# A two-layer transformer kernel on one core: the value products of its second attention done by expert, with scattered and gathered rows

## The chip, the core and the metric

The kernel runs on one core of a Trainium2 chip. The core has five engines that work side by side, each strictly through its own list of instructions: TensorE (PE, with the loading of its stationary operand shown apart as PEld), VectorE (DVE), ScalarE (ACT), GpSimd (POOL) and SyncE (SP, which issues most of the DMA transfers). The metric is the device time of one launch in microseconds (us). Runs of the same kernel stand within some tenths of a per cent of each other. Beside the plain runs there is one profiled execution, from which the views in this document come.

## The reference, cut to what matters

The input `x` has 4 sequences (`b`) of 1024 tokens with 128 numbers. Two layers follow, each of which normalizes its input and adds two branches to it. The change is in the second branch of the first layer, an attention of 8 heads with 8 experts for the values and 8 for the outputs in each head:

```python
gate_v = _get_sel_gate(x, sel_v_w, rs)      # [b, s, 8 heads, 8 experts], two experts not zero per token and head
gate_o = _get_sel_gate(x, sel_o_w, rs)
q = einsum('bsd,hpd->bhsp', x, q_w);  k = einsum('bsd,hpd->bhsp', x, k_w)
xv = einsum('bsd,hedp->bshep', x, v_w)      # every token through all 8 experts of every head
v = einsum('bshep,bshe->bhsp', xv, gate_v)  # of which the gate keeps two
att = softmax(einsum('bhqp,bhkp->bhqk', q, k) * SCALE)
ctx = einsum('bhqk,bhkp->bqhp', att, v)
out = einsum('bshep,hepd->bsd', ctx[:, :, :, None, :] * gate_o[..., None], o_w)
```

`_get_sel_gate` takes a sigmoid of the routing logits, keeps the two largest of the eight per token and head, and divides them by their sum. The first branch of the layer is an attention of 16 heads that share one key and one value. The second layer has an attention with random features and a mixture of eight experts per token (two chosen) with a shared one.

## The kernel before

A batch's 1024 tokens lie as 8 tiles of 128 rows (`NT = 8`, index `n`). The first layer is one loop over 32 units `u` (batch `b`, head `h` of the second attention), each in eight steps `n`. In a step stand, in this order: the scores of token tile `n` against all keys and their softmax (`switch_softmax`: `ss` L676, the copy L679, the maximum L681, the exponential L683), the transposes of the tile before (`switch_transpose`: `pTp` L696, copied to `pTs` L700 by DVE and by ACT), up to two outputs (`switch_output`: `po` L729, eight experts weighted on DVE L733, added up by POOL L648, L649, L738 and L739, the last into `x`), and the values of the next unit (`switch_values`). The product of probabilities and values, `switch_context` (`cp`, L708), comes in two halves: the first at step 4, the second at step 0 of the next unit. Each of a unit's values must be ready before its first half.

`switch_values` makes the values of one token tile for all eight experts: two products of 128x512 on PE (`pv`, L659), a multiplication with the gates on DVE (`gv`, L663), and three additions on POOL that sum the experts (L648, L649, L668). Six of eight gates are zero.

Between these steps the first attention is woven in, as a generator (`first_attention`) that is advanced by a fixed number of its small steps per step of the unit (`attend`, `PACE`): `mx` L451, `sT` L505, `ov` L495 and the maximum `nmh` L457 on DVE. `row_ahead` prepares the next batch (`layernorm`, `switch_gates`) from a head's first step on. When a batch is complete, `router` of the second layer writes each token to two places of a DRAM tile `sorted_x`, one indirect DMA of 128 rows at a time (`xslot` L302 on DVE, the scatter L309 on POOL).

What sets the order: PE's instructions stand in the order in which the program is written. A scheduler orders the other engines, in the first layer SyncE too; in the second layer SyncE's order is the written one as well. Tiles of a pool with a tag are reused in turn: an instruction that writes a tile waits until those that used its buffer before are done, and two transfers that write the same DRAM tile wait for each other in turn.

Of the kernel before, what the change touches and what calls it, by code (L numbers as in the profile page):

```python
# [17 lines left out]
P = 128  # L18
# [21 lines left out]

FJ = 64
# [25 lines left out]
def two_layers(ctx: ExitStack, tc: tile.TileContext, a: dict, out: bass.AP):  # L67
# [7 lines left out]
    ctx.enter_context(tc.manual_schedule(engines={mybir.EngineType.PE}))  # L75
# [94 lines left out]

    nobody = fixed([P, 2, ROW], "nobody")
# [24 lines left out]
    def layernorm(layer, b, pool):  # L196

        mv = rt.tile([P, NT, 2], F32, tag="mv", name=f"mv{layer}_{b}")
# [6 lines left out]
        rstd = rt.tile([P, NT], F32, tag="rstd", name=f"rstd{layer}_{b}")  # L205
        nc.scalar.activation(rstd, mv[:, :, 1], AF.Sqrt, bias=eps_ln)
        nc.vector.reciprocal(rstd, rstd)
        moments[b] = mv, rstd
        for q in range(NT // 4):
            xn = pool.tile([P, 4, D], F32, tag="xn", name=f"xn{layer}_{b}_{q}")  # L210
# [41 lines left out]
    def router(b):  # L252
# [45 lines left out]
        mv, rstd = moments[b]  # L298
# [19 lines left out]
    with ExitStack() as l0:  # L318
# [6 lines left out]
        def switch_gates(b):  # L325
# [25 lines left out]
            m0, oh0, m1, oh1 = found  # L351
            den = pre.tile([P, ng], F32, tag="den", name=f"den{b}")
# [7 lines left out]
            weigh(to, oh0, m0, oh1, m1)  # L360
# [3 lines left out]
            )  # L364
            yield
# [4 lines left out]
        def mqa_prepare(b):  # L370
# [13 lines left out]
            for i in range(NPART):  # L384
                if i > 0:
                    nc.vector.tensor_tensor(qf, qf, qp, ALU.subtract)
                qp = at.tile([P, T], BF16, tag="qp0", name=f"qp0_{b}_{i}")
                nc.gpsimd.tensor_copy(qp, qf)
                nc.sync.dma_start(qd[i], qp)
                yield  # L390
# [92 lines left out]
        def mqa_values(b, g):  # L483
# [3 lines left out]
            for c in range(2):  # L487
# [13 lines left out]
                for kt in range(NT):  # L501
                    pTs = []
                    for i in range(4):
# [6 lines left out]
                            [P, 512], F32, tag="pT0", name=f"pT0_{b}_{g}_{c}_{kt}_{i}", bufs=12  # L510
# [10 lines left out]
                os_ = at.tile([P, 512], F32, tag="os0", name=f"os0_{b}_{g}_{c}", bufs=1)  # L521
# [16 lines left out]
        def mqa_out(b):  # L538
# [31 lines left out]
            yield from layernorm(1, b, pre)  # L570
# [33 lines left out]
        def switch_load(u):  # L604

            b, h = divmod(u, SH)
            vw = wst.tile([P, SE, P], F32, tag="vw", name=f"vw{u}")
            ow = wst.tile([P, SE, P], F32, tag="ow", name=f"ow{u}")
            if b == 0:
                qk = wst.tile([P, 2, P], F32, tag="qk", name=f"qk{u}")  # L610
                nc.sync.dma_start(qk[:, 0, :], a["q_wT"][:, ts(h, P)])
                nc.sync.dma_start(qk[:, 1, :], a["k_wT"][:, ts(h, P)])
                unit[u, "qk"] = qk
            nc.sync.dma_start(vw, a["v_w"][ts(h, SE)].rearrange("e d p -> d e p"))
            nc.sync.dma_start(ow, a["o_w"][ts(h, SE)].rearrange("e p d -> p e d"))
            unit[u, "w"] = vw.rearrange("d e p -> d (e p)"), ow.rearrange("p e d -> p (e d)")

        def switch_scores(u):
# [7 lines left out]
            qkT = sw.tile([P, 512], F32, tag="cTs", name=f"qkT{u}")  # L626
# [8 lines left out]
        def switch_queries(u):  # L635
            b, h = divmod(u, SH)
            qT = sw.tile([P, T], F32, tag="qTs", name=f"qTs{u}")
# [13 lines left out]
        def switch_values(u, n):  # L651
# [5 lines left out]
            for c in range(2):  # L657
                pv = small(f"pv{u}_{n}_{c}")
                nc.tensor.matmul(  # L659
                    pv, lhsT=xnT[b][:, ts(n, P)], rhs=unit[u, "w"][0][:, ts(c, 512)],  # L660
# [7 lines left out]
            nc.gpsimd.tensor_tensor(v[:, n, :], g[:, 0, :], g[:, 1, :], ALU.add)  # L668

# [34 lines left out]
        def switch_context(u, qg):  # L704
# [7 lines left out]
            cT = sw.tile([P, 512], F32, tag="cTs", name=f"cTs{u}_{qg}")  # L712
# [3 lines left out]
        def switch_output(u, n):  # L716
# [10 lines left out]
            for c in range(2):  # L727
                po = small(f"po{u}_{n}_{c}")
                nc.tensor.matmul(  # L729
                    po, lhsT=cT[:, ts(qt, P)], rhs=unit[u, "w"][1][:, ts(c, 512)],  # L730
# [13 lines left out]
        weights = (3.2, 2.2, 2.2, 1.8, 3.2, 2.2, 2.2, 1.8)  # L744
# [3 lines left out]
        VALUES = {1: (0,), 2: (1,), 3: (2, 3), **LATER}  # L748
# [5 lines left out]
        def row_ahead(b):  # L754

            yield from layernorm(0, b, pre)
# [4 lines left out]
        switch_load(0)  # L761
        run(layernorm(0, 0, pre))
# [5 lines left out]
        for b in range(1, B):  # L768
            load_x(b)
        steps = first_attention()  # L770
# [3 lines left out]
        for u in range(U + 1):  # L774
            b, h = divmod(u, SH)
            for n in range(NT):
# [18 lines left out]
                if u == 0 and n == 0:  # L795
                    switch_load(1)
                elif n == 5 and u + 2 < U and u > 0 or u == 0 and n == 7:
                    switch_load(u + 2 if u else 2)
# [8 lines left out]
                if u > 0 and 1 <= n <= 3:  # L807
                    switch_output(u - 1, n + 3)
                    if n == 3:
                        switch_output(u - 1, NT - 1)  # L810
                elif u < U and n >= 5:
# [3 lines left out]
                if u > 0 or n >= 4:  # L815
                    attend(0.3)
# [665 lines left out]
```

## Time and profile before

| | |
|---|---|
| median of 3 runs | 3563.88 us (3555.51 to 3567.87) |
| the profiled execution | 3553.15 us, its span 3551.4 us |
| mean granted TensorE clock | 0.970 |
| busy: PE, DVE, ACT, POOL | 94%, 71%, 46%, 47% of the span |
| last output of the first layer (`g_o`, L738) | 3025.8 us |
| `pv` L659 / `gv` L663 / POOL's first add L648 | 487.5 / 334.6 / 328.5 us busy |

A row of a group names the line, the engine, the operation, the tile written and those read, their shapes, how often, the busy time in us and the mean of one in ns, and behind the bar the time that the engine stood idle just before and what ended it. In the rows of PE a 128x512 product in fp32 has two records. In a timeline each row begins with the start and the length in us, and ends with the idle time ahead and its releaser in brackets. The chain is the work that ended last, followed back from the end.

### The profile page before, as it was taken

To read this page: it belongs to the slowest core of one execution; us is meant where nothing else is said; L and a number is where in the kernel's file an instruction comes from. 1 tells how busy PE (TensorE), PEld (TensorE's weight loads), DVE (VectorE), ACT (ScalarE), POOL (GpSimd) and SP (SyncE) were. 2 spreads that over 40 slices of the span, in tenths; PEclk is the share of its full clock that TensorE was granted. 3 is DMA by queue.
4 is the path that set the end of the run, shared out by engine and by line. 5 is a ranking of instruction groups with operands and counts; after the bars stand their busy time and mean duration, and the time that the engine had idled before them with its cause. 6 is when DMAs were issued, how large, how long until landed. Compare 5 with 4: busy or idle time off the path is not lost.

```text
span 3551.4 us, 41035 instructions
## 1 busy us (share of the span) xinstructions
PE 3339.5 (94%) x14270; PEld 1667.4 (47%) x14270; DVE 2522.9 (71%) x4598; ACT 1642.3 (46%) x2823; POOL 1661.9 (47%) x2204
## 2 busy tenths in 40 slices
PE   5999999999989998999989999999899999889996
PEld 2444444444444443444434444444444444457775
DVE  6876678767777768676877787677777675557774
ACT  2344443444445443444444434444454445345663
POOL 3644444444465455444455454444654443303334
PEclk9999999999999998999999999999999999898998
DMA  4530101000000000000000010000000000013346
GB/s 98 153 109 14 21 14 28 6 20 13 19 23 21 12 13 22 13 19 19 14 23 19 13 28 6 20 12 20 23 21 13 7 6 1 21 35 76 77 89 149
DMA packets 174851, 116.36 MB, mean 33 GB/s; under 512 B 11754, under 2 KB 162164, under 8 KB 174644
## 3 DMA queue, kind: packets, MB, share of 16 engines
q1 hardware_dynamic: 159124, 103.29, 10.6%
q0 software_dynamic: 13280, 9.38, 1.9%
q8 instruction: 113, 1.85, 0.2%
q10 hardware_dynamic: 2240, 1.07, 0.1%
q14 instruction: 94, 0.77, 0.1%
HBM read 77.20 MB, written 36.11 MB: 32 GB/s over the span
## 4 chain that ended last, share of the span: by engine, by line
PE 77%; DVE 13%; DMA 3%; POOL 3%; issue 2%; ACT 1%; SPq 1%; DVEq 0%; POOLq 0%; ACTq 0%
PE cp L708 12%; PE ss L676 11%; PE po L729 11%; PE pv L659 11%; PE ov L495 6%; PE sT L505 5%; PE pTp L696 5%; PE mx L451 5%; DMA sorted_x<-xslot,at_slot 3%; DVE nmh L457 2%; DVE nms L681 2%; PE pe L1344 2%; PE pb L1329 2%; PE qks L640 1%; DVE gv L663 1%
## 5 line engine op out<-in xcount | busy, mean ns | idle before, releaser
L457 DVE TENSOR_REDUCE nmh<-mx 128x1 f32<-128x512 f32 x1024 | 657.4, 680 | 340.4 <-PE mx L451 339.8
L648 POOL TENSOR_TENSOR g_o<-g_o 128x512 f32<-128x512 f32 x256 | 324.8, 1269 | 1226.7 <-DVE g_o L733 1005.9
L512 ACT ACTIVATE pT<-sT 128x512 f32<-128x512 f32 x1024 | 556.6, 601 | 414.3 <-PE sT L505 410.3
L659 PE MATMUL pv<-vw,xnT 128*128 128x512 f32 x1024 | 487.5, 609 | 18.0 <-DVE pTs L700 7.8
L676 PE MATMUL ss<-xnT,qTs 128*128 128x512 f32 x1024 | 494.4, 604 | 9.8 <-DVE gv L663 6.9
L708 PE MATMUL cp<-pTs,vs 128*128 128x512 f32 x1024 | 462.9, 606 | 38.8 <-DVE pTs L700 31.6
L729 PE MATMUL po<-ow,cTs 128*128 128x512 f32 x1024 | 474.7, 596 | 2.5 <-ACT ps L679 2.5
L679 ACT COPY ps<-ss 128x512 f32<-128x512 f32 x512 | 298.4, 587 | 361.9 <-PE ss L676 340.6
L681 DVE TENSOR_REDUCE nms<-ps 128x1 f32<-128x1024 f32 x256 | 310.7, 1214 | 185.9 <-ACT ps L679 185.2
L683 ACT ACTIVATE ps<-ps,nms 128x1024 f32<-128x1024 f32 x256 | 294.3, 1150 | 180.7 <-DVE nms L681 179.6
L663 DVE TENSOR_TENSOR gv<-pv,gates 128x512 f32<-128x512 f32 x512 | 334.6, 681 | 30.6 <-POOL x L739 10.3
L648 POOL TENSOR_TENSOR gv<-gv 128x512 f32<-128x512 f32 x256 | 328.5, 1283 | 34.2 <-DVE gv L663 34.1
L733 DVE TENSOR_TENSOR g_o<-po,go 128x512 f32<-128x512 f32 x512 | 328.4, 680 | 18.9 <-PE po L729 14.2
L708 PEld LDWEIGHTS cp<-pTs,vs 128*128 128x128 f32 x1024 | 193.6, 193 | 287.2 <-issue 230.4
L451 PE MATMUL mx<-ks,qs 72*128 72x512 bf16 x1024 | 311.8, 381 | 16.4 <-DVE gv L663 6.1
L505 PE MATMUL sT<-qs,ks 75*128 75x512 bf16 x1024 | 309.9, 384 | 7.8 <-ACT pT L512 2.3
L659 PEld LDWEIGHTS pv<-vw,xnT 128*128 128x128 f32 x1024 | 195.2, 194 | 244.0 <-issue 154.6
L696 PE MATMUL pTp<-ident,ps 128*128 128x128 f32 x2048 | 270.6, 275 | 17.9 <-ACT ps L683 11.8
L676 PEld LDWEIGHTS ss<-xnT,qTs 128*128 128x128 f32 x1024 | 191.8, 192 | 201.4 <-issue 131.3
L696 PEld LDWEIGHTS pTp<-ident,ps 128*128 128x128 f32 x2048 | 239.7, 141 | 90.4 <-issue 22.7
L729 PEld LDWEIGHTS po<-ow,cTs 128*128 128x128 f32 x1024 | 180.3, 191 | 158.4 <-issue 136.5
L495 PE MATMUL ov<-pT,va 128*32 128x512 f32 x2048 | 247.5, 598 | 0.0
(270 smaller groups left out, 3999.9 us busy)
## 6 DMA issues: line engine op xcount, KB each, us to landing
w<-in_w_dram SPq DMA_DIRECT2D x78, 256.0 KB
sorted_x<-nobody SPq DMA_DIRECT2D x16, 1040.0 KB
vw<-in_v_w_dram SPq DMA_DIRECT2D x32, 512.0 KB
ow<-in_o_w_dram SPq DMA_DIRECT2D x32, 512.0 KB
qs<-qd SPq DMA_DIRECT2D x144, 64.0 KB
xg<-sorted_x SPq DMA_DIRECT2D x39, 130.0 KB
sum<-nobody SPq DMA_DIRECT2D x8, 512.0 KB
y<-sum SPq DMA_DIRECT2D x16, 256.0 KB
```

The source lines that it names most:

```text
L451: nc.tensor.matmul(sc, lhsT=qs[0:NPAIR, i, ts(n, P)], rhs=ks[0:NPAIR, ts(kc, 512)], start=True, stop=True,)
L457: nc.vector.tensor_reduce(halves[:, i, n, kc : kc + 1], sc, axis=AX.X, op=ALU.max)
L495: nc.tensor.matmul(ov[32 * i : 32 * i + 32, :], lhsT=va[:, kt, :], rhs=pT, start=(kt == 0), stop=(kt == NT - 1),)
L505: nc.tensor.matmul(sc, lhsT=ks[:, ts(kt, P)], rhs=qs[:, i, ts(c, 512)], start=True, stop=True,)
L512: nc.scalar.activation(pT, sc, AF.Exp)
L648: nc.gpsimd.tensor_tensor(g[:, 0:4, :], g[:, 0:4, :], g[:, 4:8, :], ALU.add)
L659: nc.tensor.matmul(pv, lhsT=xnT[b][:, ts(n, P)], rhs=unit[u, "w"][0][:, ts(c, 512)], start=True, stop=True,)
L676: nc.tensor.matmul(sc, lhsT=qT[:, ts(n, P)], rhs=xnT[b][:, ts(c, 512)], start=True, stop=True)
L681: nc.vector.tensor_reduce(nm, p, axis=AX.X, op=ALU.max, negate=True)
L696: nc.tensor.transpose(pt[:, ts(k, P)], p[:, ts(4 * k4 + k, P)], ident)
L708: nc.tensor.matmul(cp, lhsT=v[:, kt, :], rhs=pT[:, kt, :], start=(kt == 0), stop=(kt == NT - 1),)
L729: nc.tensor.matmul(po, lhsT=cT[:, ts(qt, P)], rhs=unit[u, "w"][1][:, ts(c, 512)], start=True, stop=True,)
```

## The change

Units 0 and 1 keep the dense values. For the other 30, a token goes only through the two experts that its gate keeps:

- Once per batch, `places` counts for each head how many tokens each expert has, rounds that up to blocks of 128 slots (at most 23 blocks for a head, `NVB`), and gives each token its two slots. The slots and the two gate weights are kept in the part of `gates` that the gates of the values had. `rows_of_values` writes the normalized tokens as rows (`xv`).
- For each unit, `scatter` writes the 8 tiles of rows to their first and second slots in a DRAM tile `sorted_v` (16 indirect DMAs from POOL; four such tiles in turn, cleared once at the start). `PAIR` says how many in which step, for two units at a time.
- In six groups of up to four blocks, `group_load` reads the blocks back and loads for each block the 128x128 weights of its expert, whose number SyncE reads into a register; `group_turn` transposes the blocks on PE, `group_product` multiplies them on PE and stores the result to a DRAM tile `yv`.
- `gather` fetches for each token tile its two rows from `yv` (16 indirect DMAs from POOL into three buffers `yg`), and DVE adds them with their weights into the values `vs`.

SyncE's order in the first layer is the written one now. To make room, the buffers of `qTs`, `qp0` and `pT0` are fewer, and several tiles share tags (`xn`, `qkT`, `xvT` with `cTs`; `os0` with `pT0`). `row_ahead` begins at head 2 instead of 5, and the second layer's first normalization of a batch waits in the program until that batch's last output is written.

```diff
+NVB = 2 * NT + SE - 1
+VG = 4
+DENSE = 2
...
-    ctx.enter_context(tc.manual_schedule(engines={mybir.EngineType.PE}))
+    ctx.enter_context(
+        tc.manual_schedule(engines={mybir.EngineType.PE, mybir.EngineType.SP})
+    )
...
+    sorted_v = [
+        hbm.tile([NVB * P, D], F32, tag=f"sorted_v{i}", name=f"sorted_v{i}") for i in range(4)
+    ]
...
             m0, oh0, m1, oh1 = found
+            if b == 0:
+                yield from rows_of_values(0)
+            slots = pre.tile([P, ng], F32, tag="top_r", name=f"slots{b}")
+            slots = slots.rearrange("p (k n h) -> p k n h", k=2, n=NT)
+            yield from places(b, gates[b], oh1.rearrange("p (n g) e -> p n (g e)", n=NT), slots)
...
+        def rows_of_values(b):
+            xv = row_of[b] = sw.tile([P, NT, D], F32, tag="xv", name=f"xv{b}", bufs=1)
+            mv, rstd = moments[0, b]
+            for n in range(NT):
+                nc.vector.tensor_scalar(
+                    xv[:, n, :], x[b][:, n, :], mv[:, n, 0:1], rstd[:, n : n + 1],
+                    ALU.subtract, ALU.mult,
+                )
...
-                qp = at.tile([P, T], BF16, tag="qp0", name=f"qp0_{b}_{i}")
+                qp = at.tile([P, T], BF16, tag="qp0", name=f"qp0_{b}_{i}", bufs=1)
...
-                            [P, 512], F32, tag="pT0", name=f"pT0_{b}_{g}_{c}_{kt}_{i}", bufs=12
+                            [P, 512], F32, tag="pT0", name=f"pT0_{b}_{g}_{c}_{kt}_{i}", bufs=10
...
+            while b not in complete:
+                yield
+            yield from layernorm(1, b, sw)
...
+        def scatter(u, i):
+            n, k = divmod(i, 2)
+            nc.gpsimd.indirect_dma_start(
+                out=sorted_v[u % 4][:, :],
+                out_offset=bass.IndirectOffsetOnAxis(ap=column(u, k, n).bitcast(I32), axis=0),
+                in_=row_of[u // SH][:, n, :], in_offset=None,
+            )
...
+        def group_load(u, g):
+            m = min(VG, NVB - VG * g)
+            if g == 0:
+                plan(u)
+            xs = sw.tile([P, VG, D], F32, tag="xs", name=f"xs{u}_{g}", bufs=3)
+            rows = unit[u, "sorted"][ds(VG * P * g, m * P), :]
+            nc.sync.dma_start(xs[:, 0:m, :], rows.rearrange("(k p) d -> p k d", p=P))
+            wb = wst.tile([P, VG, P], F32, tag="vb", name=f"vb{u}_{g}", bufs=3)
+            for i in range(m):
+                j = VG * g + i
+                e = nc.sync.value_load(
+                    unit[u, "of"][0:1, j : j + 1], min_val=0, max_val=SH * SE - 1
+                )
+                nc.sync.dma_start(
+                    wb[:, i : i + 1, :], a["v_w"][ds(e, 1)].rearrange("e d p -> d e p")
+                )
...
+        def group_turn(u, g):
+            xs, _, m = unit[u, "g", g]
+            pt = small(f"xvT{u}_{g}")
+            for i in range(m):
+                nc.tensor.transpose(pt[:, ts(i, P)], xs[:, i, :], ident)
+            xT = sw.tile([P, 512], F32, tag="cTs", name=f"xvT{u}_{g}", bufs=3)
+            nc.scalar.copy(xT[:, 0 : m * P], pt[:, 0 : m * P])
...
+        def group_product(u, g):
...
+                nc.tensor.matmul(
+                    pv[:, ts(i, P)], lhsT=xT[:, ts(i, P)], rhs=wb[:, i, :],
+                    start=True, stop=True,
+                )
+            nc.scalar.copy(xs[:, 0:m, :].rearrange("p k d -> p (k d)"), pv[:, 0 : m * P])
+            rows = unit[u, "y"][ds(VG * P * g, m * P), :]
+            nc.sync.dma_start(rows.rearrange("(k p) d -> p k d", p=P), xs[:, 0:m, :])
+
+        def gather(u, n):
...
+            for k in range(2):
+                y = sw.tile([P, P], F32, tag="yg", name=f"yg{u}_{n}_{k}", bufs=3)
+                nc.gpsimd.indirect_dma_start(
+                    out=y[:, :], out_offset=None, in_=unit[u, "y"][:, :],
+                    in_offset=bass.IndirectOffsetOnAxis(
+                        ap=column(u, k, n).bitcast(I32), axis=0
+                    ),
+                )
+                w = column(u, 2 + k, n)
+                if k == 0:
+                    nc.vector.tensor_scalar(v, y, w, None, ALU.mult)
+                else:
+                    nc.vector.scalar_tensor_tensor(v, y, w, v, ALU.mult, ALU.add)
...
+        PAIR = (
+            (1, 1, 1, 1, 1, 1, 2, 2, 2, 1, 1, 1, 1, 0, 0, 0),
+            (1, 1, 1, 1, 1, 1, 0, 0, 0, 1, 1, 1, 1, 2, 2, 2),
+        )
...
+        for i in (2, 3, 0, 1):
+            nc.sync.dma_start(
+                sorted_v[i].rearrange("(k p) d -> p k d", p=P),
+                empty.unsqueeze(1).to_broadcast([P, NVB, D]),
+            )
...
+                if h == 2 and n == 0 and b + 1 < B:
+                    aside = row_ahead(b + 1)
...
-                if u + 1 < U:
-                    for i in ({4: range(4), **LATER} if u == 0 else VALUES).get(n, ()):
-                        switch_values(u + 1, i)
+                    for i in {4: range(4), **LATER}.get(n, ()):
+                        switch_values(1, i)
+                if u == 0 and 4 <= n:
+                    for i in range(4 * (n - 4), 4 * (n - 3)):
+                        scatter(2, i)
+                if u == 1:
+                    for i in range(3 * n, min(3 * n + 3, 2 * NT)):
+                        scatter(3, i)
+                odd = u % 2
+                v = u + 3 if odd else u + 2
+                if u > 0 and v < U:
+                    for k, counts in enumerate(PAIR):
+                        done = sum(counts[: n + 8 * (1 - odd)])
+                        for i in range(done, done + counts[n + 8 * (1 - odd)]):
+                            scatter(v + k, i)
+                NG_V = -(-NVB // VG)
+                v = u + 1
+                if DENSE <= v < U:
+                    if n == 0 and v == DENSE:
+                        group_load(v, 0)
+                        group_load(v, 1)
+                    if 1 <= n <= NG_V:
+                        group_product(v, n - 1)
+                    if n < NG_V:
+                        group_turn(v, n)
+                    if n + 2 < NG_V:
+                        group_load(v, n + 2)
+                    if n == 7:
+                        gather(v, 0)
+                        gather(v, 1)
+                if DENSE <= v + 1 < U and u > 0 and n >= 6:
+                    group_load(v + 1, n - 6)
+                if DENSE <= u < U and n < 3:
+                    gather(u, 2 * n + 2)
+                    gather(u, 2 * n + 3)
```

## The prediction, made before the changed kernel ran

> **What bounds the kernel now.** The page's busy shares and the chain come first, then the windows by stage, then the groups that the change touches, last the one row that resembles what it adds.
>
> ```profile
> PE 3339.5 (94%) x14270; PEld 1667.4 (47%) x14270; DVE 2522.9 (71%) x4598; ACT 1642.3 (46%) x2823; POOL 1661.9 (47%) x2204
> PE 77%; DVE 13%; DMA 3%; POOL 3%; issue 2%; ACT 1%; SPq 1%; DVEq 0%; POOLq 0%; ACTq 0%
> 1100.00:2500.00 1400.00, 1356.14 (x5172) 624.50 (x5171) 1023.08 (x1759) 644.39 (x1155) 698.60 (x915) 0.98 0.07 17
> L659 PE MATMUL pv<-vw,xnT 128*128 128x512 f32 x1024 | 487.5, 609 | 18.0 <-DVE pTs L700 7.8
> L663 DVE TENSOR_TENSOR gv<-pv,gates 128x512 f32<-128x512 f32 x512 | 334.6, 681 | 30.6 <-POOL x L739 10.3
> L648 POOL TENSOR_TENSOR gv<-gv 128x512 f32<-128x512 f32 x256 | 328.5, 1283 | 34.2 <-DVE gv L663 34.1
> ```
>
> In the window from 1100 to 2500 us (columns: PE, PEld, DVE, ACT, POOL busy, clock, DMA share, GB/s) PE works 97% of the time, DVE 73%, POOL 50%, ACT 46%: PE paces the first layer. The first layer's outputs end at 3025 us; with the start off, 32 units take about 92.3 us each, 11.5 us for each of a unit's eight steps. The values cost PE, DVE and POOL alike.
>
> **PE.** Removed per unit: 32 records of L659. In the PE timeline four of them start and the next group follows 1.71 us later, so 0.43 us a record, 13.7 us a unit (by the busy mean, which overlaps, more). Added: 23 transposes, eight of which follow at 0.87 to 1.09 us, so 2.7 us; 23 products of 128x128, two records each, by the row of `pe` (L1344: 81.7 us for 624 records) 0.26 us each, 6.0 us. Saved: about 5 us a unit, 30 units, 150 us. Where PE paces, a unit takes 87.5 us.
>
> **DVE and ACT.** DVE loses 16 `gv` of 681 ns (10.9 us) and gains 16 weighted sums of 128x128, priced by the `xslot` row (346 ns): 5.5 us. ACT gains 12 copies of 587 ns (L679): 7 us on 42. `places` adds some 35 DVE operations a batch of 0.2 to 0.35 us, about 10 us; DVE is idle 27% of the time and hides it after batch 0. None of these is late by its sum.
>
> **SyncE.** 23 `value_load`s (269, 152 and 18 ns) and as many weight loads (42, 29 and 378 ns): 0.9 us a block, 20 us a unit, with the group transfers 24. That fits in 87. They are loaded two groups ahead. An `xs` load waits in order on its scatters' landing, and queued behind it are `qs` loads for the first attention; I give that nothing at best and 2 us a unit at worst, and take nothing.
>
> **POOL.** Removed: eight add chains of 2.6 us a unit, 21 us. Kept: eight output chains, 3.17 us each (1028.36 to 1031.53 in the timeline), 25.4 us. Added: 16 scatters and 16 gathers, each issued by POOL. The row of a scatter of rows (who waited for it below it), and its queue in the timeline:
>
> ```profile
> L309 POOL DMA_INDIRECT sorted_x<-xslot,at_slot x64: 968/992/2053, 1014.8 to 3114.2; - x64
>   DVE xslot L302: 60.1, 48
> DMA to landing us min/median/max: 2.3/2.3/3.4
> ```
>
> ```profile
> 1014.81 1.31 POOL L309 DMA_INDIRECT sorted_x<-xslot,at_slot  x1 [0.85 <-issue]
> 1017.77 1.00 POOL L309 DMA_INDIRECT sorted_x<-xslot,at_slot  x1 [1.66 <-DMA sorted_x<-xslot,at_slot]
> 1028.09 0.19 POOL L307 COPY xslot<-token 128x1 int32<-128x1 int32 x1
> 1028.21 0.18 POOL L308 COPY xslot<-share 128x1 f32<-128x1 f32 x1
> 1028.36 1.25 POOL L648 TENSOR_TENSOR g_o<-g_o 128x512 f32<-128x512 f32 x1
> 1031.07 0.46 POOL L739 TENSOR_TENSOR x<-x,g_o 128x128 f32<-128x128 f32 x1
> 1031.78 1.00 POOL L309 DMA_INDIRECT sorted_x<-xslot,at_slot  x1 [0.25 <-issue]
> 3085.56 0.97 POOL L309 DMA_INDIRECT sorted_x<-xslot,at_slot  x1 [1.80 <-DVE xslot L302]
> 3088.63 0.98 POOL L309 DMA_INDIRECT sorted_x<-xslot,at_slot  x1 [1.80 <-DMA sorted_x<-xslot,at_slot]
> ```
>
> A scatter alone costs POOL 1.0 us and 0.25 us of issue: 1.25 (the one after the chain). A scatter right behind another into the same DRAM tile waits for that one's landing, because the two are ordered as writes: start to start 2.96 and 3.07 us. The new scatters are of this kind: all 16 of a unit go to one `sorted_v` tile. In the changed kernel's POOL order 272 of the 480 follow another scatter directly, some nine of 16 in a plain unit. No row shows a gather; as a lower bound I take a scatter with nothing to wait for, 1.25, as an upper one the same plus the landing with three in flight (2.3 + 1.0 + 0.35 of DVE + 0.7 of release, over three buffers: 1.45); I take 1.27. A plain unit on POOL:
>
> 25.4 (outputs) + 16 x 1.27 (gathers) + 7 x 1.25 + 9 x 3.07 (scatters) + 1.5 (small) = 84 us.
>
> So POOL goes from 50% to 96% of a PE-paced unit, and it works strictly in order. [...]
>
> **Not all units are plain.** POOL by unit, by its order and the prices above: units 5, 13 and 21 hold 30 scatters (116 us), units 4, 12 and 20 only two (49), units 11, 18, 19 and 26 the router's scatters too (106 to 119; before, those cost too: the 60.1 us above), units 28 to 31 none (46).
>
> **Order.** The weighted sums stand on DVE where the schedule put them. In most plain units those of gathers 0 to 3 of the next unit stand *ahead* of the copy of the last transposes (`pTs`, L700 before) of the present one, which the second context product (`cp`, L708 before) needs at step 0 of the next unit. Walk unit 8 on POOL from its predecessor's last output chain, at step 3: eight scatters in a row (1.25 + 7 x 3.07 = 22.7 us), two output chains with four scatters among and behind them (3.2 + 3.2 + 1.3 + 2.0 + 6.1), one more scatter, three gathers and another (6.3), a chain begun, a scatter, a gather (5): 50 us, 56 with the waits for outputs that arrive a step at a time. Then 10 us to the eighth gather and 3 to its landing: 63 to 69 us. PE wants that copy some five steps after step 3, at 54. DVE stands still at the weighted sum meanwhile, PE behind it: a stall of 9 to 15 us, I take 12. A plain unit then lasts 87.5 + 12 = 99.5, 7.2 us more than before. Nine of 26 units have a kinder order (the copy ahead of all or most of those sums), so the bounds are none and 12 for each.
>
> **The start.** Before, PE reached the first attention at 83 us and ran without gaps from 104:
>
> ```profile
> 72.61 8.73 PE L659 MATMUL pv<-vw,xnT 128*128 128x512 f32 x16 [3.93 <-DVE gv L663]
> 82.90 0.60 PE L451 MATMUL mx<-ks,qs 72*128 72x512 bf16 x2
> 103.45 0.60 PE L451 MATMUL mx<-ks,qs 72*128 72x512 bf16 x2
> ```
>
> After: `gates_0` has `places` and eight rows of `xv` ahead (some 13 us), 6 MB of clears stand ahead of `qd` and `qs` on SyncE, and POOL's order has 16 scatters among unit 0's chains and 49 more, round the four tiles so that they do not wait for each other (1.25 each: 61 us), ahead of unit 1's first add chain. Unit 1 is dense; its `gv` has three buffers, so DVE stops at the fourth, and PE behind it, until POOL is through: 13 + 16 x 1.25 + 61 = 94 us at worst, 40 if `places` and half of the queue hide. I take 90.
>
> **The sum, to the profiled execution** (3553.15 us, 10.7 under the median of 3563.88, 0.3%, and about what this kernel's measurement can tell from no change: 0.3% is some 11 us).
> With all stalls: 15 plain units x 7.2 = +108; units 5, 13, 21 at 116 against 92.3, +72; four router units +12 each (112 against 92.3, less the part that they paid before), +48; units 4, 12, 20 and 28 to 31 gain 5 each, -35; start +90; `places` in the open +8: +291, 3844 us.
> With POOL's sums but no stall of DVE in plain units: 15 x -5 instead, -75: +108, 3661 us.
> I take the middle, 3750 us: which takes the walk as right for half of the stalls.
>
> **Rivals.** (1) *As meant*: POOL's work slides beside PE, PE paces, -150 at +20 to +90 for the start: 3423 to 3493. For it: POOL's 84 us are under 87.5, heavy units have light neighbours (116 + 49 for two). Against it: POOL waits in order and has no slack to catch up. Decides if the copy of `pTs` is on time, that is, gather 3 lands within 54 us of step 3. (2) *Balance*: the saved 150 us pay for the start and the heavy units: 3540 to 3570. For it: the sum without stalls is only 108 from there, and the start may cost 40. (3) *SyncE late as well*: an `xs` load that waits for late scatters holds the `qs` loads behind it, the first attention's operands arrive late, and PE waits once a unit more, 4 to 8 us: 3844 + 30 x 4 to 8 = 3960 to 4080. For it: SyncE already waits long on PE's releases in this layer, and its DMAs are issued in order. Against it: 63 us of it are free per unit. That the change does not do what it says is excluded: in the new order the dense products stay in units 0 and 1 alone.
>
> **Chances.** Forecast (3580 to 3900) 0.57; rival 1 0.22; rival 2 0.06; rival 3 0.15. Faster by over 0.3%: 0.22; within: 0.05; slower: 0.73. The range leaves out the far half of rival 3 and the foot of rival 1: 3440 to 3950.
>
> **What would show it.** Right: POOL's share at 80% or more, with scatter waiting on DMA; PE under 92%; a new group of DVE idle time at the weighted sums, released by the gathers' DMA, 200 us or more; PE's `cp` waiting on `pTs`; PE's steady work beginning near 190 us; scatter pitch 3.1. Wrong: PE still at 97% in the windows, DVE's waits on gathers under 50 us, or scatters in a row at 1.3 us.

## The result and the profile after

| | median | runs | profiled execution | clock |
|---|---|---|---|---|
| before | 3563.49 us | 4 (3555.51 to 3567.87) | 3553.15 us | 0.970 |
| changed | 4017.89 us | 4 (4003.51 to 4021.76) | 4017.88 us, span 4016.0 | 0.897 |

The ratio is 1.1271, with an interval of 1.1236 to 1.1305: slower by 12.7%, and 68 us above the predicted range. From the page of the changed kernel:

```profile
PE 3306.0 (82%) x15396; PEld 1792.1 (45%) x15396; DVE 2441.8 (61%) x4891; ACT 1821.1 (45%) x3181; POOL 2008.7 (50%) x2453
PE 39%; DMA 21%; POOL 17%; DVE 13%; issue 8%; ACT 1%; SPq 1%; POOLq 0%; DVEq 0%; ACTq 0%
L818 POOL DMA_INDIRECT sorted_v<-xv,gates x480 | 471.3, 982 | 579.6 <-DMA sorted_v<-xv,gates 463.0
L871 POOL DMA_INDIRECT yg<-yv,gates x480 | 462.2, 963 | 170.6 <-issue 73.0
L879 DVE TENSOR_SCALAR vs<-yg,gates 128x128 f32<-128x128 f32 x240 | 87.5, 367 | 363.8 <-DMA yg<-yv,gates 363.6
L881 DVE SCALAR_TENSOR_TENSOR vs<-yg,gates,vs 128x128 f32<-128x128 f32 x240 | 105.0, 438 | 254.9 <-DMA yg<-yv,gates 254.7
```

No engine is full: PE is down from 94% to 82%, and POOL, where the chain now spends 17% and the transfers it waits for most of another 21%, stands at 50%. The third group says why: POOL's 480 scatters cost 471 us of work and 463 us of standing until the scatter before has landed. DVE, strictly in order too, stands 618 us (363.6 + 254.7) at the weighted sums until the gathered rows land.

PE's busy time fell by only 33.5 us (3339.5 to 3306.0), and its idle time in the span rose from 211.9 to 710.0 us. In the middle of the first layer (columns as before):

```profile
1000.00:3000.00 2000.00, 1670.66 (x7306) 852.92 (x7305) 1233.11 (x2497) 936.64 (x1705) 1091.94 (x1351) 0.91 0.26 72
```

PE works 84% of this window instead of 97%, at a granted clock of 0.91 instead of 0.98. Who waits for whom (total, times, longest, in us):

```profile
POOL g_o L766 <- DVE g_o L946: 539.9, 90, 19.7
POOL sorted_v L818 <- DMA sorted_v<-xv,gates: 463.0, 256, 6.9
DVE vs L879 <- DMA yg<-yv,gates: 363.6, 168, 15.6
PE mx L557 <- DVE nmh L563: 103.8, 27, 15.5
PE sT L611 <- DVE nmh L563: 92.2, 11, 19.0
PE cp L921 <- DVE pTs L913: 48.1, 19, 10.4
```

Read together they look like a ring: POOL waits for DVE's weighted outputs (`g_o`), DVE for the rows that POOL gathers, and PE for DVE: mostly for the maxima of the first attention (`nmh`), and for 48 us for the copy `pTs`. Two of them say little alone, for the kernel before had them too:

```profile
POOL g_o L648 <- DVE g_o L733: 1005.9, 156, 19.2
PE cp L708 <- DVE pTs L700: 31.6, 28, 3.2
```

There POOL's 1005.9 us were time that it had to spare. So the way from DVE back to POOL is not shown by these totals. The way from POOL over DVE to PE is, in one stretch of an ordinary unit, first on POOL:

```profile
1057.93 0.72 POOL L767 TENSOR_TENSOR g_o<-g_o 128x256 f32<-128x256 f32 x1
...
1059.87 0.98 POOL L818 DMA_INDIRECT sorted_v<-xv,gates  x1 [0.15 <-issue]
1061.16 0.97 POOL L871 DMA_INDIRECT yg<-yv,gates  x1 [0.30 <-issue]
1062.44 0.96 POOL L871 DMA_INDIRECT yg<-yv,gates  x1 [0.31 <-issue]
...
1076.76 0.97 POOL L871 DMA_INDIRECT yg<-yv,gates  x1 [0.16 <-issue]
```

then on DVE:

```profile
1064.37 0.33 DVE L879 TENSOR_SCALAR vs<-yg,gates 128x128 f32<-128x128 f32 x1 [7.35 <-DMA yg<-yv,gates]
...
1072.15 1.31 DVE L881 SCALAR_TENSOR_TENSOR vs<-yg,gates,vs 128x128 f32<-128x128 f32 x1 [2.55 <-DMA yg<-yv,gates]
...
1079.33 0.35 DVE L881 SCALAR_TENSOR_TENSOR vs<-yg,gates,vs 128x128 f32<-128x128 f32 x1 [3.10 <-DMA yg<-yv,gates]
```

and on PE:

```profile
1059.51 0.38 PE L611 MATMUL sT<-qs,ks 75*128 75x512 bf16 x1
1065.31 0.58 PE L611 MATMUL sT<-qs,ks 75*128 75x512 bf16 x1 [5.42 <-DVE g_o L946]
...
1068.16 3.64 PE L889 MATMUL ss<-xnT,qTs 128*128 128x512 f32 x4 [1.41 <-DVE nmh L563]
...
1082.79 0.58 PE L611 MATMUL sT<-qs,ks 75*128 75x512 bf16 x1 [6.38 <-DVE nmh L563]
...
1084.87 8.89 PE L921 MATMUL cp<-pTs,vs 128*128 128x512 f32 x16
...
1094.47 1.88 PE L889 MATMUL ss<-xnT,qTs 128*128 128x512 f32 x4
```

A gather that POOL starts at 1061 after its scatters holds DVE from about 1057 to 1064; the output multiplication behind it (1064.57) is late, and PE stops for 5.42 us. A second stop of 6.38 us follows 11 us later, when the rows of the gather of 1076.76 release DVE at 1079.33. The four `ss` products that follow the first stop take 3.64 us; the same four take 1.88 at 1094.47.

**By unit**, taken between the second halves of `cp`: the second half of the first unit starts at 232.0 us instead of 133.7 (+98). The 31 units that follow take 3247 us instead of 2867 (+380): units 1 to 3 +51, units 4 to 27 +327 (108.2 us each instead of 94.6), units 28 to 31 +3. The second layer takes 14 us less (536.7 instead of 550.5). The start shows its cause in two rows:

```profile
198.30 1.29 DVE L781 TENSOR_TENSOR gv<-pv,gates 128x512 f32<-128x512 f32 x2 [65.49 <-POOL vs L786]
199.05 0.58 PE L557 MATMUL mx<-ks,qs 72*128 72x512 bf16 x1 [59.13 <-DVE gv L781]
```

DVE and PE stand until POOL adds up unit 1's dense values (`vs`); 64 scatters start on POOL before 232 us.

### The profile page after: what moved, and what is told of

Read it like the earlier page. It is cut to its first block, busy times and chain, and to the rows that moved or that the text cites. A ratio compares the mean times of both kernels' runs of the same rounds, so it can differ in the third digit from the quotient of the medians.

```text
span 4016.0 us, 49975 instructions
## 1 busy us (share of the span) xinstructions
PE 3306.0 (82%) x15396; PEld 1792.1 (45%) x15396; DVE 2441.8 (61%) x4891; ACT 1821.1 (45%) x3181; POOL 2008.7 (50%) x2453
## 4 chain that ended last, share of the span: by engine, by line
PE 39%; DMA 21%; POOL 17%; DVE 13%; issue 8%; ACT 1%; SPq 1%; POOLq 0%; DVEq 0%; ACTq 0%
DMA sorted_v<-xv,gates 10%; DMA yg<-yv,gates 7%; PE cp L921 6%; PE po L942 6%; PE ss L889 5%; POOL sorted_v L818 5%; POOL yg L871 3%; POOL g_o L766 3%; PE pTp L909 2%; PE ov L601 2%; PE sT L611 2%; PE mx L557 2%; DVE nmh L563 2%; PE pg L856 2%; DMA sorted_x<-xslot,at_slot 2%
## 5 line engine op out<-in xcount | busy, mean ns | idle before, releaser
L563 DVE TENSOR_REDUCE nmh<-mx 128x1 f32<-128x512 f32 x1024 | 658.9, 681 | 213.4 <-PE mx L557 211.9
L818 POOL DMA_INDIRECT sorted_v<-xv,gates x480 | 471.3, 982 | 579.6 <-DMA sorted_v<-xv,gates 463.0
L921 PE MATMUL cp<-pTs,vs 128*128 128x512 f32 x1024 | 503.6, 649 | 71.0 <-DVE pTs L913 48.1
L871 POOL DMA_INDIRECT yg<-yv,gates x480 | 462.2, 963 | 170.6 <-issue 73.0
L942 PE MATMUL po<-ow,cTs 128*128 128x512 f32 x1024 | 491.0, 612 | 17.9 <-DVE nmh L563 15.8
L909 PEld LDWEIGHTS pTp<-ident,ps 128*128 128x128 f32 x2048 | 256.9, 150 | 253.8 <-DVE nmh L563 89.1
L921 PEld LDWEIGHTS cp<-pTs,vs 128*128 128x128 f32 x1024 | 209.8, 211 | 326.4 <-issue 256.7
L909 PE MATMUL pTp<-ident,ps 128*128 128x128 f32 x2048 | 293.8, 289 | 63.1 <-DVE nmh L563 54.6
L879 DVE TENSOR_SCALAR vs<-yg,gates 128x128 f32<-128x128 f32 x240 | 87.5, 367 | 363.8 <-DMA yg<-yv,gates 363.6
L881 DVE SCALAR_TENSOR_TENSOR vs<-yg,gates,vs 128x128 f32<-128x128 f32 x240 | 105.0, 438 | 254.9 <-DMA yg<-yv,gates 254.7
L915 ACT COPY pTs<-pTp 128x512 f32<-128x512 f32 x256 | 148.5, 580 | 237.7 <-PE pTp L909 231.4
```

What stands on the lines that cost most here:

```text
L563: nc.vector.tensor_reduce(halves[:, i, n, kc : kc + 1], sc, axis=AX.X, op=ALU.max)
L818: nc.gpsimd.indirect_dma_start(out=sorted_v[u % 4][:, :], out_offset=bass.IndirectOffsetOnAxis(ap=column(u, k, n).bitcast(I32), axis=0), i ...
L871: nc.gpsimd.indirect_dma_start(out=y[:, :], out_offset=None, in_=unit[u, "y"][:, :], in_offset=bass.IndirectOffsetOnAxis(ap=column(u, k, n ...
L909: nc.tensor.transpose(pt[:, ts(k, P)], p[:, ts(4 * k4 + k, P)], ident)
L921: nc.tensor.matmul(cp, lhsT=v[:, kt, :], rhs=pT[:, kt, :], start=(kt == 0), stop=(kt == NT - 1),)
L942: nc.tensor.matmul(po, lhsT=cT[:, ts(qt, P)], rhs=unit[u, "ow"][:, ts(c, 512)], start=True, stop=True,)
```

## The experiments

The theory after this reading: POOL's order brings the gathers late, DVE stops at the sums behind them, and PE behind DVE. Against it stood three others: that the rows of scatters waiting for each other's landing are the cause by themselves; that POOL and the DMA queues are simply overloaded, wherever DVE waits; and that other parts of the change cost the time, SyncE's written order above all. The kernel before took 3557 to 3563 us beside every one of these runs.

**1. POOL's order written**, so that the scheduler no longer gathers scatters into rows.

```diff
-        tc.manual_schedule(engines={mybir.EngineType.PE, mybir.EngineType.SP})
+        tc.manual_schedule(engines={mybir.EngineType.PE, mybir.EngineType.SP, mybir.EngineType.Pool})
```

> POOL's order in the first layer is the written one, as PE's and SyncE's are; nothing else is changed, so scatters of two units alternate and stand between output chains. Theory (order on POOL: scatters stand in a row and wait for each other's landing, gathers come late, DVE stands still at the weighted sums and PE behind it): the scatters' wait for a scatter falls from 463 us to under 200, DVE's waits for gathers from 618 us to under 300, the first half of unit 0's second context product is at 150 us instead of 232, time 3580 to 3750 us. Rival A (POOL's load as such, 480 scatters and 480 gathers, whatever the order): 3900 to 4020. Rival B (SyncE's written order and the transfers that it issues late): 3950 to 4050.

Measured: 4120.11 us, ratio 1.1564 (1.1539 to 1.1589). Its waits:

```profile
POOL g_o L766 <- DVE g_o L946: 705.0, 129, 18.8
DVE vs L879 <- DMA yg<-yv,gates: 559.0, 218, 20.3
DVE vs L881 <- DMA yg<-yv,gates: 117.6, 135, 2.8
POOL sorted_v L818 <- DMA sorted_v<-xv,gates: 209.9, 136, 4.6
```

The expectation failed, in the time, in DVE's waits for gathers (677 us, under 300 expected) and in the start (the second half of the first unit's `cp` at 198 us, 150 expected). The scatters' standing fell by more than half, to just above the 200 expected, and the kernel got slower. In the written order a gather stands behind the output chain of its step, which waits for DVE, which waits for the gather before: DVE and POOL go in lockstep, and both of their waits grew. So rows of scatters are not the cause by themselves. Some 47 us of this time lie in the second layer (584 us instead of 537), where POOL's written order held as well.

**2 to 4. The transfers left out**, one kind at a time and both.

```diff
         def scatter(u, i):
             n, k = divmod(i, 2)
+            return                                  # 2 and 4
...
-                y = sw.tile([P, P], F32, tag="yg", name=f"yg{u}_{n}_{k}", bufs=3)
-                nc.gpsimd.indirect_dma_start(out=y[:, :], ...)
+                y = ident                           # 3 and 4
```

> Leaves out the 480 scatters (the blocks are read from the cleared tiles); all else stays. Theory: POOL has 46 us of work in a unit, gathers are on time, DVE waits for them under 150 us; time 3430 to 3600 us. Rival A: the same, 3450 to 3600. Rival B: within 80 us of 4018.

> Leaves out the 480 gathers (the weighted sums read a constant tile instead); all else stays, the scatters in a row too. Theory: DVE has nothing to wait for, the scatters only have to be done a unit ahead, which they are; the start keeps its 95 us; time 3480 to 3620 us. Rival A: 3600 to 3800. Rival B: within 80 us of 4018.

> Leaves out scatters and gathers. What is left is the rest of the change: PE's saving of 5 us a unit, SyncE's order and loads, ACT's copies, the smaller buffers. Theory: PE paces again, 3551 - 150 and 20 for the start: 3400 to 3460 us, clock 0.96 or more. Rival B: 3850 or more, SyncE's or ACT's waits on the path.

| | time (runs 2 to 4: a single run each) | above run 4 |
|---|---|---|
| 4: neither | 3418.61 us | |
| 3: scatters alone | 3563.66 us | 145 |
| 2: gathers alone | 3650.19 us | 232 |
| the changed kernel | 4017.89 us | 599 |

Run 4 keeps SyncE's written order, its loads and register reads, the products by expert, ACT's copies and the smaller buffers, and it is 145 us faster than the kernel before. SyncE's order and the rest of the change are not the cause. Run 4 has no scatters for an `xs` load to wait for, so the prediction's rival 3 falls by run 3: there the scatters stand 530 us for each other, and it takes 3564 us. In the changed kernel, too, PE waits only 1.4 us in all for `qs` loads. Runs 3 and 4 came out as expected; run 2 did not: it is 50 us above its range, and DVE still waits 335 us for gathers (under 150 expected). So gathers come late without any scatter as well. Run 4's page and its middle window:

```profile
PE 3166.4 (93%) x15396; PEld 1731.8 (51%) x15396; DVE 2428.7 (71%) x4891; ACT 1819.1 (53%) x3179; POOL 1080.0 (32%) x1493
```

```profile
900.00:2700.00 1800.00, 1718.20 (x7849) 885.42 (x7848) 1321.58 (x2665) 1007.70 (x1838) 566.86 (x819) 0.98 0.23 63
```

PE is back at 95% of the window and at 0.98. It executes the same 15396 products as the changed kernel, yet is busy for 3166.4 us in run 4 and 3306.0 in the changed kernel: 139.6 of the 599 us are the same work done more slowly (the median of an `ss` record is 592 ns in both), and 459.6 (710.0 - 250.4) are idle time. Each kind of transfer alone costs 145 or 232, both together 222 more than their sum: the two kinds get in each other's way. Whether that is their order or their load on POOL, this table can't tell; runs 5 to 11 test it.

**5. Everything issued, but the sums read a constant tile**, so DVE never waits for a gather.

```diff
-                    nc.vector.tensor_scalar(v, y, w, None, ALU.mult)
+                    nc.vector.tensor_scalar(v, ident, w, None, ALU.mult)
...
-                    nc.vector.scalar_tensor_tensor(v, y, w, v, ALU.mult, ALU.add)
+                    nc.vector.scalar_tensor_tensor(v, ident, w, v, ALU.mult, ALU.add)
```

> Everything is issued as in the changed kernel, scatters and gathers too, but DVE's weighted sums read a constant tile, so that DVE never waits for a gather. POOL's load is unchanged. Theory C (the cost is made where DVE, in order, stands at a weighted sum behind a gather and PE behind DVE; POOL's load alone costs little): 3560 to 3640 us, near the 3564 without gathers. Rival A (POOL's load as such delays the output chains and so PE): 3800 or more. The start stays at some 95 us in both.

Measured: 3680.51 us, a single run: 40 us above the range of the theory and far under the rival's 3800. POOL does all of its work in it, and its standing has hardly changed:

```profile
PE 3218.3 (87%) x15396; PEld 1750.3 (48%) x15396; DVE 2424.6 (66%) x4891; ACT 1817.2 (49%) x3179; POOL 2011.2 (55%) x2453
```

```profile
POOL sorted_v L818 <- DMA sorted_v<-xv,gates: 443.9, 249, 6.3
```

So 337 us go when DVE need not stop at the sums, with POOL as loaded as before. (Nor do the gathers wait here for DVE to free their buffers; in the changed kernel those waits are 26 us.) Plain units take 82 to 90 us. What is left above run 4 (262) is the start (the second half of the first unit's `cp` still at 232) and the units beside the heavy and the router's scatters (106 to 134). There POOL's own work is late: DVE waits 81 us for POOL's sums of the dense values (`vs`), 52 for `qp` and 42 for the last step of the outputs (`x`), where run 4 has 4 or 5 for each.

**6. The sums one step later**, behind the step's maximum, the first row gathered straight into `vs`.

```diff
+                y = v
+                if k == 1:
+                    y = sw.tile([P, P], F32, tag="yg", name=f"yg{u}_{n}", bufs=3)
+                    late.append((u, n, y))
...
+        def weigh_rows(nm):        # called at the end of switch_softmax; z = 0 * nm binds it there
...
+            for u, n, y in late:
+                v = unit[u, "v"][:, n, :]
+                nc.vector.tensor_scalar(v, v, column(u, 2, n), z, ALU.mult, ALU.add)
+                nc.vector.scalar_tensor_tensor(v, y, column(u, 3, n), v, ALU.mult, ALU.add)
```

> The sums of a step's gathers are written one step later and bound to that step's maximum (they add zero times it), and the first of a token's two rows is gathered straight into the values' tile, so the three buffers serve the second row alone. POOL's order stays the scheduler's. Theory C: the sums come some 5 us later than before but the gathers are still behind scatters in a row; half of the wait goes: 3750 to 3900 us. Rival A: 3950 or more, since POOL's load is the same.

Measured: 3846.31 us, a single run, as expected: 172 us less for moving DVE's sums and for gathering half of the rows past the three buffers; which of the two gives how much is not shown.

**7 to 9. Gathers ahead of the output chain, sums later still.** Run 7 writes POOL's order, issues a step's gathers before its outputs, binds the sums to the next step's copy of the transposes, gives `yg` four buffers (room comes from `pastv` in bf16) and lets scatters alternate with other work in `PAIR`. Run 8 is the same with POOL left to the scheduler and the old `PAIR`; run 9 is run 7 with POOL's order written in the first layer only.

```diff
-            (1, 1, 1, 1, 1, 1, 2, 2, 2, 1, 1, 1, 1, 0, 0, 0),
-            (1, 1, 1, 1, 1, 1, 0, 0, 0, 1, 1, 1, 1, 2, 2, 2),
+            (1, 1, 1, 1, 1, 1, 1, 1, 2, 1, 1, 2, 1, 1, 0, 0),
+            (1,) * 16,
...
+                if DENSE <= u < U and n < 3:          # moved up from below the outputs
+                    gather(u, 2 * n + 2)
+                    gather(u, 2 * n + 3)
                 if u > 0 and 1 <= n <= 3:
                     switch_output(u - 1, n + 3)
```

> POOL's order written; a step's four gathers stand ahead of its output chain, scatters of two units alternate, the sums of the gathers are bound to the copy of the next step's transposes (so never ahead of it), four buffers for the second rows, the first rows gathered into the values' tile. Theory C: neither engine waits for the other within a step; a unit is near the 83 us that it has without scatters and gathers, the start near that of the written POOL order: 3440 to 3600 us. Rival A (load): 3800 or more.

> As the one before, but POOL's order and the scatters' turns as in the changed kernel (scheduler's). Theory C: sums never stand ahead of the copy of the transposes, gathers still late behind scatters in a row: 3650 to 3850 us. Rival A: 3800 or more.

> As the kernel with early gathers, but POOL's written order ends with the first layer (before, it went on in the second, whose part took 584 us against 537 in the changed kernel). Theory: the second layer's 45 to 50 us come back and nothing else changes: 3615 to 3640 us. If the second layer is slower for another reason: 3660 or more.

Measured: 3674.16, 3775.27 and 3612.01 us, a single run each. Run 7 missed its range although its plain units take 81 to 88 us, near the expected 83, and its start is that of run 1 (second half at 197): the other units (up to 121 us, the mean of units 4 to 27 is 95.5) and the 584 us of the second layer had not been counted. Run 8 was in its range and 101 us slower than run 7. Run 9 is 62 us faster than run 7, 51 of them in the second layer (533 us instead of 584), and 3 us under its range. Against run 8 it is 163 us faster: POOL's order and the scatters' turns in the first layer are worth that much, once the sums no longer make it a lockstep.

**10, 11 and 15. Four dense units instead of two**, so that the first scatters are not in a hurry: on the changed kernel (10), and on run 9's (11, and again as 15).

```diff
-DENSE = 2
+DENSE = 4
...
```

The rest of the edit loads the dense weights of units 2 and 3, makes their values over a unit's steps, and drops the scatters and group loads that stood for them in units 0 and 1.

> The changed kernel with four dense units in place of two; scatters begin in unit 1. Orders of POOL and DVE are the scheduler's. Theory (the start is lost to scatters ahead of unit 1's add chains): the first half of unit 1's context product moves from 266 us to under 215, the whole from 4018 to 3930 to 3985 us (less the PE saving of two units). If the start is lost to the clears or to the gates: within 15 us of 4018.

> Early gathers with POOL's written order in the first layer alone, and four dense units. Theory: plain units at 82 to 88 us, start 50 us shorter than with two dense units: 3540 to 3600 us, about the time of the kernel before; the rest over the 3419 without scatters and gathers is in the units that hold a batch's router scatters, and in the start. Rival A (POOL's load): 3650 or more.

> The same kernel as e11 (3572 us there), on the same chip as the next run. If the 11 us a plain unit of the last three runs are their edits': 3565 to 3580 us. If they are the chip's that those runs fell on, this run may show them too: 3720 to 3750, with ACT's copy of the second context product released by nothing that the profile shows.

Measured: 3983.3 us, a single run; 3572.49 us, ratio 1.0029 (1.0013 to 1.0045); 3573.99 us, ratio 1.0033 (1.0018 to 1.0047). Run 10's time lies in its range by luck: it kept the late start (the second half at 234 us, the first half of unit 1 at 271 and not under 215), since the scheduler hoists the scatters of unit 4 just as it did those of unit 2, 64 of them before 234 us. Its gain is in units 1 to 3, which take 272 us instead of 311. In run 11, with POOL's order written, no scatter starts before the second half, which comes at 166. Run 11 is 445 us under the changed kernel with nearly the same scatters and gathers (448 of each instead of 480). DVE waits 130 us for gathers instead of 618, and the scatters stand 116 us for each other instead of 463, though POOL is busy for 56%, more than in the changed kernel:

```profile
POOL sorted_v L823 <- DMA sorted_v<-xv,gates: 115.5, 69, 6.2
DVE vs L895 <- DMA vs<-yv,gates: 103.3, 49, 10.2
DVE vs L896 <- DMA yg<-yv,gates: 27.0, 30, 4.7
```

**12 to 14 and 16. The router's scatters spread**, one per step of the generator instead of four (13 and 16), batch 0's rows made after the gates (14), or both (12), all on run 11's kernel.

```diff
                     in_=xn[:, :], in_offset=None,
                 )
-            if n % 2:
                 yield
```

> The kernel with early gathers and four dense units, and two edits more: the router yields after every scatter instead of every fourth, so that a batch's 16 scatters to the other tile spread over more steps, and batch 0's rows are written after its gates. Theory (what is left over the kernel without scatters and gathers is POOL's queue in the three units that hold those scatters, 124, 136 and 116 us against 105, 109 and 89, and the start): each of the three loses 10 to 15 us, the start 3: 3525 to 3550 us, 0.3 to 1% under the kernel before. If those units are long for DVE's other work on the batch change: 3565 to 3580.

> Early gathers, four dense units, and the router's yield after every scatter; batch 0's rows written where they were. If the 11 us that each plain unit lost in the run before come with the rows' place: plain units back at 82 to 86 us, the three router units at 114, 127 and 114 us as there, 3525 to 3555 us. If they come with the router's spread: plain units at 94 us, 3730 to 3760.

> Early gathers, four dense units, batch 0's rows written after its gates; the router as it was. If the 11 us come with the rows' place: plain units at 94 us, 3740 to 3775 us. If with the router's spread: plain units at 83, 3560 to 3575.

> The same kernel as e13 (3724 us there). If the chip decides, it stands with the run before on the same side, 10 to 30 us shorter for the router's spread: 3540 to 3565 or 3700 to 3735. If the spread itself costs the 11 us: 3720 to 3750 beside 3572.

Measured: 3746.45 us, ratio 1.0522 (1.0501 to 1.0544); 3723.93, ratio 1.0461 (1.0442 to 1.0479); 3744.48 (a single run); and, for the kernel of run 13 on another chip, 3550.8, ratio 0.9975 (0.9958 to 0.9991). Run 12 lies far above both of its ranges, run 13 just under the one for a cost of the router's spread (3730 to 3760), and run 14 in the one for the rows' place (3740 to 3775). Yet that is not shown to be the edits' doing: the same program took 3724 us on one chip (run 13) and 3551 on another (run 16), while the kernel before took 3560 on both. Run 13's page of waits holds rows that run 16's has none of:

```profile
DVE nmh L567 <- remote: 47.4, 10, 10.4
ACT cTs L942 <- remote: 46.6, 5, 13.1
```

"Remote" means a release that the profile can't name. Plain units take 93 to 98 us in run 13 and 83 to 88 in run 16. What this is stays open: run 11's kernel was not run on the chips of runs 12 to 14, so comparing these with it says nothing on the edits, and run 14's was not run on another. Runs 15 and 16 shared a chip: there the router's spread saves 23 us, as expected. Neither the changed kernel nor any of runs 1 to 11 has such rows, so the 454 us of this change are not that. Run 16 is the fastest version that computes everything, 0.25% under the kernel before, which is within what this measurement can tell from no change; a gain of the size of run 4's was not reached.

## Why the prediction was right and wrong

**Right: direction and mechanism.** POOL in order, late gathers, DVE's head of the line, PE behind it: the stretch above shows the links, and runs 5, 6 and 11 that most of the time goes with them. One link is wider than predicted: gathers are late without scatters too (run 2); in run 1 they stand behind the output chains. The start was priced at +90 and measured at +98, for the reason given. The three heavy units were seen, and their price was right; in the division used here they lie one unit earlier than named: units 4, 12 and 20 hold 30, 32 and 32 scatters and take 113, 121 and 118 us (116 predicted). Of the signs named, the late steady start (199 us), PE under 92% and DVE idle at the sums by 200 us or more (618) came true; `cp` waiting on `pTs` hardly did.

**The step that failed is "takes the walk as right for half of the stalls".** The middle between 3661 and 3844 had no row behind it. The walk's own figure was good: 12 us a unit against 5.42 + 1.41 + 6.38 = 13.2 us in the stretch shown. But units 4 to 27 see-saw between 83 and 136 us, and the 14 plain ones among them (11 to 22 scatters, none of the router's) take 103.2 us on average, above even the 99.5 of a plain unit with its whole stall. The reason given for the half was that in nine units `pTs` stands ahead of the sums. By the waits, PE stops elsewhere: at the first attention, whose maxima (`nmh`) are on DVE behind the same sums (196 us of waits for them by `mx` and `sT`, 48 for `pTs`, of which 32 were there before). The place of `pTs` was no cover.

**Even the sum with all stalls, 3844, is 174 us short.** A second term failed there: it put the speed of PE's work behind a stop at its old value, without a reason. The sum's terms against the measured units:

- Units 4 to 27: +327 where that sum had +206 (14 plain ones at 7.2, 72 for the heavy, 48 for the router's, -15 for the three with next to no scatters). Against run 4, the same 9446 products keep PE busy 101 us longer in these units (windows below), which is most of the missing 121. PE's idle time is 342 us longer; the sum had some 326 there (206 and the 5 us saved in each of the 24 units). So the stalls, taken in full, were sized nearly right.
- Units 28 to 31, without scatters: +3 in place of -20. They still gather, and DVE still waits.
- Units 1 to 3: +51, for which `places` (+8) and the plain price stood. Units 2 and 3 take 113 and 107 us, as long as later ones: they were no exception to the stalls. (The sum also counts 15 plain units where its own list leaves 16: 26 units with scatters less 3, 4 and 3. That is 7 us.)
- The start is 8 over, the second layer 14 under.

The windows of units 4 to 27, first in the changed kernel, then in run 4:

```profile
543.19:3140.78 2597.59, 2168.93 (x9446) 1104.87 (x9445) 1570.22 (x3142) 1211.52 (x2209) 1416.72 (x1728) 0.91 0.27 75
421.70:2577.00 2155.30, 2068.19 (x9446) 1063.83 (x9446) 1562.97 (x3133) 1208.87 (x2206) 667.51 (x955) 0.98 0.24 67
```

PE's saving was sized well: in run 4 units 4 to 27 take 89.8 us each where the kernel before takes 94.6, 4.8 us less (predicted 5). The stalls hide it.

**POOL's price.** The scatter behind a scatter was taken at 3.07 us from the router's scatters (L309); it is 2.49 in the rows below (2.51 in the median). From the timeline:

```profile
1038.79 0.96 POOL L818 DMA_INDIRECT sorted_v<-xv,gates  x1 [1.53 <-DMA sorted_v<-xv,gates]
1041.27 0.96 POOL L818 DMA_INDIRECT sorted_v<-xv,gates  x1 [1.53 <-DMA sorted_v<-xv,gates]
```

The scatters' median here is 2.3 us from issue to landing, and the next starts 2.49 us after it, some 0.6 us less than in the row chosen. A gather takes 1.25 us from start to start (as from 1078.03 to 1079.28), as predicted (1.27). With these the prediction's sum for a plain unit falls from 84 to 78 us. The POOL share of 80% was wrong as a sign: the profile's busy share counts work, 50%, and not the standing, which was priced into those 84 us. Nor did POOL's sum set the pace of the plain units: run 5 does the same POOL work in 82 to 90 us, where the changed kernel takes 103. What counts there is when the gathers come.

**Rival 3** (3960 to 4080) holds the measured time by number alone: its cause is excluded by run 3 and by PE's waits for `qs` loads (1.4 us). **Rival 1** was close on what the change is worth without its transfers (3423 to 3493 forecast, 3418.61 in run 4) and wrong in that POOL's work does not slide beside PE.

## What to carry to other kernels

When a change gives an engine that works in order both the producing of rows and a chain that waits for their consumer, look at the order first, and at whether the two engines can come to wait for each other, as in run 1: the sum of the work says little (here 50% busy, and 445 us recovered at 56%). Cover for a late row is only what stands *between* the row's consumer and the next thing anybody needs from the consumer's engine; list all of those, not just the nearest. And price each stop twice: the idle time, and the slower work behind it (here 459.6 and 139.6 us of the 599 above run 4). To find out what an added kind of work costs, leave out each kind alone and both together: a cost above the sum (here 599 against 145 + 232 us) says that they get in each other's way, and a run with the same work in another order (here run 11) says how much of it is order.

## What the runs showed of the hardware

- In the stretch of the changed kernel shown above, PE's products run at half speed for a while behind a stop: four `ss` behind the stops of 5.42 and 1.41 us take 3.64 us instead of 1.88 (as at 1094.47), sixteen `cp` behind the stop of 6.38 us 8.89 instead of 7.03 (as at 1026.78). After the stop of 6.38 us, from 1082.79 to about 1088.3, record follows record at twice the usual distance (0.85 us instead of 0.43 for a 128x512 product in fp32), so some 2.8 us are lost. The changed kernel has 59 idle times of PE of 3 us or more, a bound chosen for the count, and run 4 has 15; by an estimate from the 2.8 us of this one stretch, the 44 more would cost 123 of the 139.6 us above. How long a stop must be for this, and what sets the length of the slow time, is not shown. The mean granted clock is 0.897 in the changed kernel and 0.963 in run 4. Over the kernel the slower work is 3.5% (139.6 of 4016.0).
- One program, two chips: 3724 and 3551 us (runs 13 and 16), with the kernel before at 3560 on both; the cause is not known. By this pair, two kernels should be compared on one chip, and a kernel before that runs at its usual time there does not show that the chip treats the other one as usual.
- In the changed kernel 128 rows of 512 bytes cost POOL 0.97 us of work to scatter and 0.95 to gather, in the median of 480 each, and land after 2.3 and 2.5 us.
